# Layer 2's first chunks gather raw rows, moments are taken block by block, table blocks leave the filling, and idle TensorE multiplies for nobody

## The chip, the cores and the metric

One core of a Trainium2 chip runs the whole kernel. The core has five engines that work side by side, each through its own instruction queue and in order: PE (TensorE, matrix products and transposes), DVE (VectorE), ACT (ScalarE), POOL (GpSimd) and SP (SyncE, which here issues transfers only). The metric is the time of one execution on the device, in microseconds (us).

## The reference

A graph with N = 6250 nodes of D = 128 features and 106,250 edges (50,000 in both directions and one loop per node), sorted by destination. Two layers of a graph transformer with two heads are applied, with a batch normalisation and a ReLU between them, and the result is added to the input and normalised:

```python
def _transformer_conv(h, edge_attr, src, dst, Wq, bq, Wk, bk, Wv, bv, We, Ws, bs):
    q = (h @ Wq + bq).reshape(n, H, C)
    k = (h @ Wk + bk).reshape(n, H, C)
    v = (h @ Wv + bv).reshape(n, H, C)
    e = (edge_attr @ We).reshape(-1, H, C)
    kj = k[src] + e
    alpha = jnp.einsum('ehc,ehc->eh', q[dst], kj) / jnp.sqrt(jnp.asarray(C, h.dtype))
    ...
    a = ex / den[dst]          # softmax over the edges of one destination
    out = jax.ops.segment_sum((v[src] + e) * a[:, :, None], dst, num_segments=n)
    return out.reshape(n, H * C) + h @ Ws + bs
...
rel_t_enc = jnp.cos(rel_t[:, None] * time_w[None, :] + time_b)
edge_attr = jnp.concatenate([rel_t_enc, msg], axis=-1)
h = _transformer_conv(x, edge_attr, ..., Wq1, ...)
mu = h.mean(axis=0)
var = ((h - mu) ** 2).mean(axis=0)
h = jax.nn.relu((h - mu) / jnp.sqrt(var + 1e-05) * bn_g + bn_b)
return _transformer_conv(h, edge_attr, ..., Wq2, ...)
...
x = _layernorm(x + gnn(x, ...), axis=-1)
```

The mean and the variance of the normalisation run over all nodes, so no value of layer 2 can be formed before the last node of layer 1 is done. What can be done before is anything that works on the raw rows h.

## The kernel before

**Chunks.** The edges are cut into 107 chunks (NC) of 1024 edges, each of eight tiles of 128. A chunk covers a window of 64 destination nodes (NN). The function conv(c, extra) does one layer, c = 0 or 1, as a loop over rounds k from -4 to 109. It is a pipeline written out by hand: the program order is the order on every engine. In round k:

- fetch(k+4): SP loads the chunk's edge attributes into the buffer ff (L720) and its part of the table into ftab (L731); in layer 2 also the stored time code, the turned edge features and the residual rows (L734 to L738). DVE fills some columns of ff (L723 in layer 2, L726 to L729 in layer 1).
- gather(k+4): POOL issues eight indirect transfers (L743), each of which fetches the source rows of 128 edges: in layer 1 from xv_d (the input with its time), in layer 2 from h_d (layer 1's rows after normalisation and ReLU).
- score(k), L809/L810: PE multiplies the table by the turned features; lowest(k), L815/L817: DVE takes a bound; weigh(k), L822: ACT's exponential, once in a round.
- turn_weights(k-1), L832/L833, and gather_sums(k-1), L839: the weights are turned (PE, then ACT) and multiply the gathered rows; the sums are in fpa, a single bank.
- divide(k-2), L844 to L847; finish_turn(k-2), L853 to L856; finish(k-2): two products (L863/L864), in layer 1 a DVE addition (L869) and a transfer of the 64 columns into hT, the layer's result, which lies in SBUF with the features on partitions; in layer 2 L887 to L891 and the output.
- turn_in(k+1), L792/L793 and for layer 1 L799: PE transposes the gathered rows, ACT copies them.
- in layer 1, encode and sine form the time code of a chunk two or three rounds ahead (L760 to L768 on DVE, a sine on ACT), place copies it into ff (L779).
- pull(extra, 1): one step of side work.

Buffers of a chunk (ff and ftab) are there six times, so the gathers of a layer's first six chunks can run one after the other, and the seventh waits until the first chunk's sums (L839) have read their buffer. This stretch, rounds -4 to -1, is called the filling here.

**Side work.** A table holds, for a block of 512 nodes, what score needs of the destinations: tables() makes five products of 128x512 (L627), whose results ACT (L631 twice, L629) and DVE (L633 twice) write into fo, and one transfer writes fo, 1.5 MB, to tab_d (L637). There are 13 blocks. In layer 1 block 0 is made before the loop and blocks 1 to 12 are steps of rest(), five to a block, with small loads (load_others) after block 2 and the folded weights of layer 2 (matrices) behind the last. Six steps are pulled in round -4 and one in each round after. In layer 2 a block has the table and the residual (h @ Ws + bs, added to the input, L1030 to L1032, written to res_d).

**Between the layers** (L975 to L1046): POOL clears hT's tail; the sum over the nodes, half on DVE, half on ACT (L983); the squares on ACT (L988); scale and shift; then for each block ReLU with scale and shift on ACT (L1003), four transposes on PE (L1006), a copy on DVE (L1008, four buffers fhr) and a transfer into h_d. Then the tables and residuals of blocks 0 and 1 with one PSUM bank, then conv(1), whose first gathers wait for h_d.

## Time and profile before

| | us |
|---|---|
| median of 9 runs | 2882.65 |
| lowest and highest of them | 2842.16, 2895.57 |
| the profiled execution | 2869.65 |
| its span in the profile | 2867.5 |
| mean granted clock of PE in it | 0.941 of full |
| first and last exponential (L822) of layer 1 | 120.3, 1464.4 |
| last transfer into hT landed | 1477.6 |
| first gather of layer 2 | 1508.1 |
| first and last exponential of layer 2 | 1582.9, 2844.7 |

Times are counted from the start of the span. A group line of the page gives line, engine, operation, output <- input, the count, then busy time, mean ns of one, and the idle time of the engine just before such instructions with what ended most of it. A matmul on PE has a record for its product and one (PEld) for the loading of its weights. An indirect transfer is counted on POOL for the time in which POOL writes its descriptors. The clock row (PEclk) shows in 40 slices which share of its full clock PE was granted.

### The profile page before, as it was taken

How to read it: one execution, taken by the hardware profiler on the slowest of the kernel's cores; microseconds unless marked ns; L12 is line 12 of the kernel's file. 1: busy time of each engine (PE TensorE's matmuls, PEld its weight loads, DVE VectorE, ACT ScalarE, POOL GpSimd, SP SyncE). 2: the span in 40 equal slices, each digit the busy share in tenths (PEclk: the TensorE clock that was granted, in tenths of full speed). 3: DMA queues.
4: the chain of work that ended last, by engine and by line, in shares of the span. 5: the costliest groups of instructions: out<-in, count | busy, mean ns of one | idle time of the engine just before them, and what ended most of it. 6: DMA issues, size and time to landing. Idle time of an engine off the chain costs nothing.

```text
span 2867.5 us, 39250 instructions
## 1 busy us (share of the span) xinstructions
PE 2387.0 (83%) x11637; PEld 1761.5 (61%) x11637; DVE 1242.9 (43%) x3735; ACT 1236.2 (43%) x1950; POOL 1636.9 (57%) x1733
## 2 busy tenths in 40 slices
PE   5588898888888888888864989889988888888887
PEld 3366666666666666666651656666666666666665
DVE  3455566555556565655531333333333222232223
ACT  2355665544454444544451334333333333333334
POOL 4355565555556566666606466666666666666661
PEclk7799999999999999999985999999999999999998
DMA  6345555554455455455424555565555454544451
GB/s 196 116 116 146 139 153 149 138 145 139 138 161 143 128 135 134 133 133 134 134 79 133 167 149 160 151 167 150 157 155 151 132 130 129 137 133 133 128 134 48
DMA packets 428354, 396.58 MB, mean 138 GB/s; under 512 B 282064, under 2 KB 371940, under 8 KB 424804
## 3 DMA queue, kind: packets, MB, share of 16 engines
q1 hardware_dynamic: 354406, 238.66, 30.2%
q0 software_dynamic: 55168, 114.12, 16.2%
q10 hardware_dynamic: 18558, 41.20, 4.0%
q8 instruction: 95, 1.56, 0.2%
q14 instruction: 127, 1.04, 0.1%
HBM read 279.72 MB, written 110.59 MB: 136 GB/s over the span
## 4 chain that ended last, share of the span: by engine, by line
PE 33%; issue 6%; another core or an unknown queue 4%; DVE 3%; POOL 2%; DMA 1%; ACT 1%; SPq 0%; DVEq 0%; ACTq 0%; POOLq 0%
PE fpa L839 11%; PE fps L809 5%; PE fps L810 5%; PE fppt L832 3%; PE fpx L792 3%; POOL ff L743 2%; PE fpg L627 1%; PE fpo L875 1%; PE fpo L853 1%; PE fpo L876 1%; DMA ff<-h_d,fsrcs 1%; DVE fa L847 1%; PE fpo L854 0%; DVE flow L815 0%
## 5 line engine op out<-in xcount | busy, mean ns | idle before, releaser
L743 POOL DMA_INDIRECT ff<-xv_d,fsrcs x856 | 821.6, 960 | 596.4 <-issue 224.3
L743 POOL DMA_INDIRECT ff<-h_d,fsrcs x856 | 810.2, 946 | 521.6 <-issue 252.2
L839 PE MATMUL fpa<-ff,fpt 128*128 128x225 f32 x3424 | 709.6, 360 | 0.2
L839 PEld LDWEIGHTS fpa<-ff,fpt 128*128 128x128 f32 x3424 | 641.8, 193 | 13.5 <-issue 0.9
L809 PE MATMUL fps<-fft,ftab 128*128 128x512 f32 x856 | 463.2, 620 | 90.0 <-ACT fs L822 45.3
L793 ACT COPY fft<-fpx 128x512 f32<-128x512 f32 x428 | 250.1, 584 | 527.3 <-PE fpx L792 191.5
L832 PEld LDWEIGHTS fppt<-fident,fs 128*128 128x128 f32 x1712 | 204.5, 141 | 200.2 <-issue 195.1
L832 PE MATMUL fppt<-fident,fs 128*128 128x128 f32 x1712 | 251.3, 276 | 83.0 <-issue 81.0
L833 ACT COPY fpt<-fppt 128x512 f32<-128x512 f32 x428 | 227.1, 581 | 129.0 <-PE fppt L832 55.8
L792 PE MATMUL fpx<-fident,ff 128*128 128x128 f32 x1712 | 261.6, 290 | 14.9 <-DVE fbits L726 13.5
L822 ACT ACTIVATE fs<-fps,fm 128x1024 f32<-128x1024 f32 x214 | 238.7, 1115 | 68.5 <-issue 29.8
L815 DVE TENSOR_REDUCE flow<-fps 128x1 f32<-128x1024 f32 x214 | 260.0, 1215 | 13.3 <-PE fps L810 13.3
L891 ACT ACTIVATE fsq<-fy 64x128 f32<-64x128 f32 x107 | 33.1, 310 | 505.2 <-DVE fy L889 310.4
L887 DVE SCALAR_TENSOR_TENSOR fres<-fpo,fr 64x128 f32<-64x128 f32 x107 | 30.2, 282 | 506.5 <-PE fppt L832 196.2
L809 PEld LDWEIGHTS fps<-fft,ftab 128*128 128x128 f32 x856 | 170.8, 228 | 127.8 <-issue 67.1
L810 PE MATMUL fps<-fxT,ftab 112*128 112x512 f32 x428 | 228.9, 613 | 6.2 <-issue 5.4
L792 PEld LDWEIGHTS fpx<-fident,ff 128*128 128x128 f32 x1712 | 216.9, 151 | 20.1 <-DVE fbits L726 15.1
L810 PE MATMUL fps<-fet,ftab 112*128 112x512 f32 x428 | 222.8, 601 | 0.3 <-issue 0.3
L799 ACT COPY fet<-fpe 112x512 f32<-112x512 f32 x214 | 126.5, 591 | 223.4 <-PE fppt L832 80.4
L856 DVE COPY fat<-fpo 128x256 f32<-128x256 f32 x214 | 90.9, 425 | 254.6 <-PE fpo L854 107.8
L853 PEld LDWEIGHTS fpo<-fident,fa 128*128 128x128 f32 x214 | 30.8, 144 | 269.3 <-issue 155.1
L853 PE MATMUL fpo<-fident,fa 128*128 128x128 f32 x214 | 65.6, 307 | 139.2 <-DVE fa L847 92.6
(198 smaller groups left out, 2549.8 us busy)
## 6 DMA issues: line engine op xcount, KB each, us to landing
ff<-in_edge_attr SPq DMA_DIRECT2D x214, 256.0 KB
et_d<-fet SPq DMA_DIRECT2D x107, 448.0 KB
fxT<-et_d SPq DMA_DIRECT2D x107, 448.0 KB
ftab<-tab_d SPq DMA_DIRECT2D x107, 192.0 KB
tab_d<-fo ACTq DMA_DIRECT2D x13, 1536.0 KB
ff<-xv_d,fsrcs POOLq DMA_INDIRECT x856
enc_d<-fzs SPq DMA_DIRECT2D x107, 128.0 KB
ff<-h_d,fsrcs POOLq DMA_INDIRECT x856
```

Of the source, the lines that this page charges most:

```text
L743: nc.gpsimd.indirect_dma_start(out=f[:, t, (1 if c else 0):1 + D], out_offset=None, in_=h_d if c else pl.xv_d, in_offset=bass.IndirectOffs ...
L792: nc.tensor.transpose(px[:, t * P:(t + 1) * P], s.f[:, u * 4 + t, 1:1 + D], ident)
L793: nc.scalar.copy(s.ft[:, u * GE:(u + 1) * GE], px)
L799: nc.scalar.copy(s.et[:, u * GE:(u + 1) * GE], pe[:EC])
L809: nc.tensor.matmul(s.ps[:, w], s.tab[:, :, 0], s.ft[:, w], start=True, stop=False)
L810: nc.tensor.matmul(s.ps[:, w], s.tab[:EC, :, 1], s.et[:, w], start=False, stop=True)
L815: nc.vector.tensor_reduce(low, s.ps, AX.X, OP.min)
L822: nc.scalar.activation(s.s, s.ps, AF.Exp, bias=s.bias, scale=-1.0)
L832: nc.tensor.transpose(pp[:, t * P:(t + 1) * P], s.s[:, at:at + P], ident)
L833: nc.scalar.copy(s.pt[:, u * GE:(u + 1) * GE], pp)
L839: nc.tensor.matmul(s.pa, s.pt[:, t * P:(t + 1) * P], s.f[:, t, 1:1 + D + EW], start=t == 0, stop=t == T - 1)
L853: nc.tensor.transpose(s.po[:, 0], s.a[:, :D], ident)
```

## The change

**Raw rows.** While layer 1 still runs, the finished columns of hT are turned into rows and written to h_d before any normalisation (pass_rows: four transposes, a DVE copy, one transfer per block; a block is passed when no later chunk can write to it, by the test on at_round: blocks 0 to 9 in rounds 84 to 92, block 10 in round 100, blocks 11 and 12 in rounds 108 and 109). The chunks 0, 1 and 2 of layer 2 (RAW = 3) gather these raw rows. For them turn_in applies the ReLU with scale and shift in ACT's copy out of PSUM, and normalise(k) does the same to the rows in ff with three DVE operations over 128x1024, by a tile (spread) that holds scale and shift along the free axis, made with two products. All other chunks gather from a second buffer, hn_d, which first_blocks writes: the ReLU of blocks 1 to 12, then for all 13 blocks transposes, copy and transfer. It stands in layer 2's round -4, behind fetch(0) and gather(0).

**Moments.** In pass_rows DVE takes bn_stats of the block; bn_aggr joins the 13 results, in place of the two passes over hT.

**Tables.** No step is pulled before round 0. From there one in a round, two in rounds 0 to 3 and from 81 on. Each block has two steps more that hold nothing or one of the small loads; the rows follow as further steps. fo and fzs have one buffer instead of two. In layer 2 only block 0 is made ahead of the loop, with three banks; the blocks 1 to 12, each with two empty steps, are steps of the rounds.

**Products that nobody reads.** keep_busy(n) issues n products of 128x225 on PE: 8 near the start of the plan (the index work before the layers), 12 behind the first table, 24 in round -1 of either layer ahead of turn_in(0), and 24 each in rounds 108 and 109 of layer 1. Those of round 108 stand ahead of finish(106), the layer's last chunk.

The memset of hT's tail moves to the start. The diff, cut:

```diff
 def tables(nc, pl, c, fT, b0, work, bank):
-    o = work.tile([P, GE, H, 3 - c], F32, name="fo", tag="fo")
+    o = work.tile([P, GE, H, 3 - c], F32, name="fo", tag="fo", bufs=1)
     for i, (a, b) in enumerate(pl.mats[c]):
...
     h_d = dram.tile([N, D], F32, name="h_d")
+    hn_d = dram.tile([N, D], F32, name="hn_d")
+    at_round = [0]
+    stats = const.tile([P, -(-N // GE), 6], F32, name="fstats")
     res_d = dram.tile([NP, D], F32, name="res_d")
     enc_d = dram.tile([NC, P, T * TD], F32, name="enc_d")
...
     SINGLE = 24
-    def conv(c, extra):
+    RAW = 3
+    def conv(c, extra, first_blocks=None):
         cs = ExitStack()
...
                 nc.gpsimd.indirect_dma_start(
-                    out=f[:, t, (1 if c else 0):1 + D], out_offset=None, in_=h_d if c else pl.xv_d,
+                    out=f[:, t, (1 if c else 0):1 + D], out_offset=None, in_=(h_d if k < RAW else hn_d) if c else pl.xv_d,
                     in_offset=bass.IndirectOffsetOnAxis(ap=pl.srcs[:, t, k:k + 1], axis=0))
         shape = [P, T, TD]
...
             args.clear()
-            z = work.tile([P, 2, T, TD], F32, name="fzs")
+            z = work.tile([P, 2, T, TD], F32, name="fzs", bufs=1)
             nc.scalar.activation(z[:, :len(of)], arg[:, :len(of)], AF.Sin, bias=qpi)
             turned.extend((k, z[:, i]) for i, k in enumerate(of))
...
                 nc.tensor.transpose(px[:, t * P:(t + 1) * P], s.f[:, u * 4 + t, 1:1 + D], ident)
-            nc.scalar.copy(s.ft[:, u * GE:(u + 1) * GE], px)
+            if c and k < RAW:
+                nc.scalar.activation(s.ft[:, u * GE:(u + 1) * GE], px, AF.Relu, bias=pl.shift, scale=pl.scale)
+            else:
+                nc.scalar.copy(s.ft[:, u * GE:(u + 1) * GE], px)
             if c:
...
             nc.vector.tensor_scalar(s.a, s.pa, inv, None, op0=OP.mult)
+        def normalise(k):
+            rows = ch[k].f[:, :, 1:1 + D]
+            for i, op in enumerate((OP.mult, OP.add)):
+                nc.vector.tensor_tensor(rows, rows, pl.spread[:, None, i].to_broadcast([P, T, D]), op)
+            nc.vector.tensor_scalar(rows, rows, 0.0, None, op0=OP.max)
         def finish_turn(k):
             s = ch[k]
...
             if j > NC - 3:
                 nc.sync.dma_start(tail_d[bass.ds(at - base, NN), :], o)
+        def keep_busy(n):
+            idle = p_a.tile([P, D + EW], F32, name="fpa")
+            for _ in range(n):
+                nc.tensor.matmul(idle, ident, pl.even, start=True, stop=True)
         def pull(gen, n):
...
                     gather(k + AHEAD)
-                if k == -AHEAD and c == 0:
-                    pull(extra, 6)
+                if k == -AHEAD and c:
+                    first_blocks()
                 if on(k):
...
                     lowest(k)
+                if k == -1 or c == 0 and k > NC:
+                    keep_busy(24)
                 if on(k + 1):
...
                             sine()
-                pull(extra, 1)
+                if k >= 0:
+                    at_round[0] = k
+                    pull(extra, 2 if k < 4 or k > 80 else 1)
                 if len(args) == 3 or args and k == NC - 4:
...
                 if c and on(k):
+                    if k < RAW:
+                        normalise(k)
                     nc.vector.tensor_copy(ch[k].f[:, :, 1 + D:1 + D + TD], ch[k].z)
...
                     gather_sums(k - 1)
+            at_round[0] = 2 * NC
             for _ in extra:
...
             turn_features(nc, pl, mp, N)
+        def pass_rows(b0):
+            r0 = b0 * GE
+            n = min(GE, N - r0)
+            rows = turned_rows(b0)
+            nc.vector.bn_stats(stats[:, b0], hT[:, r0:r0 + n])
+            yield
+            put_rows(h_d, b0, rows)
+            yield
+        def turned_rows(b0):
+            r0 = b0 * GE
+            n = -(-min(GE, N - r0) // P)
+            pt = pl.bank().rearrange("p (b d) -> p b d", d=P)
+            for i in range(n):
+                nc.tensor.transpose(pt[:, i], hT[:, r0 + i * P:r0 + (i + 1) * P], ident)
+            rows = pw.tile([P, GE // P, P], F32, name="fhr")
+            nc.vector.tensor_copy(rows[:, :n], pt[:, :n])
+            return rows
+        def put_rows(to, b0, rows):
+            r0 = b0 * GE
+            n = min(GE, N - r0)
+            full = n // P
+            if full:
+                nc.sync.dma_start(to[r0:r0 + full * P, :].rearrange("(b p) d -> p b d", p=P), rows[:, :full])
+            if n > full * P:
+                nc.sync.dma_start(to[r0 + full * P:N, :], rows[:n - full * P, full])
         def rest():
+            others = load_others(nc, pl, const, conv2, bn_g, bn_b)
             for b0 in range(1, NT):
                 yield from tables(nc, pl, 0, xT[:, b0 * GE:(b0 + 1) * GE], b0, pw, lambda: pl.bank())
-                if b0 == 2:
-                    yield from load_others(nc, pl, const, conv2, bn_g, bn_b)
+                for _ in range(2):
+                    next(others, None)
+                    yield
             yield from matrices(nc, pl, 1, const, lambda: pl.bank()[:, :P])
+            for b0 in range(-(-N // GE)):
+                while at_round[0] < 3 + max(k for k in range(NC) if first(k)[0] < (b0 + 1) * GE):
+                    yield
+                yield from pass_rows(b0)
         conv(0, rest())
-    nc.gpsimd.memset(hT[:, N:], 0.0)
-    with tc.tile_pool(name="fbn1", bufs=1) as one, tc.tile_pool(name="fbnw", bufs=2) as pw:
-        neg = one.tile([P, 2], F32, name="fmu")
-        half = N // 2
-        scr = pl.xT
-        nc.vector.tensor_reduce(neg[:, 0:1], hT[:, :half], AX.X, OP.add)
-        nc.scalar.activation(scr[:, half:N], hT[:, half:N], AF.Copy, accum_out=neg[:, 1:])
-        mu = one.tile([P, 1], F32, name="fmu1")
-        nc.vector.tensor_add(mu, neg[:, 0:1], neg[:, 1:])
-        nc.vector.tensor_scalar(mu, mu, -1.0 / N, None, op0=OP.mult)
-        var = one.tile([P, 1], F32, name="fbvar")
-        nc.scalar.activation(scr[:, :N], hT[:, :N], AF.Square, bias=mu, accum_out=var)
-        nc.vector.tensor_scalar(var, var, 1.0 / N, EPS, op0=OP.mult, op1=OP.add)
-        nc.scalar.activation(var, var, AF.Sqrt)
-        scale = one.tile([P, 1], F32, name="fscale")
-        nc.vector.reciprocal(scale, var)
+        moments = const.tile([P, 2], F32, name="fmom")
+        nc.vector.bn_aggr(moments, stats)
+        std = const.tile([P, 1], F32, name="fstd")
+        nc.vector.tensor_scalar(std, moments[:, 1:], EPS, None, op0=OP.add)
+        nc.scalar.activation(std, std, AF.Sqrt)
+        scale = pl.scale = const.tile([P, 1], F32, name="fscale")
+        nc.vector.reciprocal(scale, std)
         nc.vector.tensor_mul(scale, scale, pl.bng)
-        shift = one.tile([P, 1], F32, name="fshift")
-        nc.vector.tensor_mul(shift, scale, mu)
-        nc.vector.tensor_add(shift, shift, pl.bnb)
-        NB = -(-N // P)
-        with tc.tile_pool(name="fbnh", bufs=4) as hp, \
-                tc.tile_pool(name="fbnp", bufs=2, space=bass.MemoryType.PSUM) as pps:
-            for b0 in range(0, NB, 4):
-                n = min(4, NB - b0)
-                cs_ = slice(b0 * P, b0 * P + GE)
-                nc.scalar.activation(hT[:, cs_], hT[:, cs_], AF.Relu, bias=shift, scale=scale)
-                pt = pps.tile([P, 4, P], F32, name="fpt")
-                for i in range(n):
-                    nc.tensor.transpose(pt[:, i], hT[:, (b0 + i) * P:(b0 + i + 1) * P], ident)
-                hr = hp.tile([P, 4, P], F32, name="fhr")
-                nc.vector.tensor_copy(hr[:, :n], pt[:, :n])
-                full = min(n, (N - b0 * P) // P)
-                if full:
-                    nc.sync.dma_start(h_d[b0 * P:(b0 + full) * P, :].rearrange("(b p) d -> p b d", p=P), hr[:, :full])
-                if full < n:
-                    left = N - (b0 + full) * P
-                    nc.sync.dma_start(h_d[(b0 + full) * P:N, :], hr[:left, full])
+        shift = pl.shift = const.tile([P, 1], F32, name="fshift")
+        nc.vector.tensor_mul(shift, scale, moments[:, 0:1])
+        nc.vector.tensor_sub(shift, pl.bnb, shift)
         def residual(b0):
...
             next(res, None)
             yield
-        with tc.tile_pool(name="fpp2", bufs=1, space=bass.MemoryType.PSUM) as pp:
+        def relu(b0):
+            r = slice(b0 * GE, (b0 + 1) * GE)
+            nc.scalar.activation(hT[:, r], hT[:, r], AF.Relu, bias=shift, scale=scale)
+        def first_blocks():
+            for b0 in range(1, NT):
+                relu(b0)
+            for b0 in range(-(-N // GE)):
+                put_rows(hn_d, b0, turned_rows(b0))
+        with tc.tile_pool(name="fpp2", bufs=3, space=bass.MemoryType.PSUM) as pp, tc.manual_schedule():
             pl.bank = lambda: pp.tile([P, GE], F32, name="fpg")
-            for b0 in range(2):
-                for _ in block(b0):
-                    pass
+            relu(0)
+            for _ in block(0):
+                pass
+            diag = const.tile([P, 2, P], F32, name="fdiag")
+            spread = pl.spread = const.tile([P, 2, P], F32, name="fspread")
+            pb = pp.tile([P, 2, P], F32, name="fpb", bufs=1)
+            for i, col in enumerate((scale, shift)):
+                nc.vector.tensor_scalar(diag[:, i], ident, col, None, op0=OP.mult)
+                nc.tensor.matmul(pb[:, i], pl.ones, diag[:, i], start=True, stop=True)
+            nc.vector.tensor_copy(spread, pb)
         def rest():
-            for b0 in range(2, NT):
+            for b0 in range(1, NT):
                 yield from block(b0)
-        conv(1, rest())
+                yield
+                yield
+        conv(1, rest(), first_blocks)
     nc.sync.dma_start(out[N - NN:N, :], tail_d[NN:2 * NN, :])
...
         got.hT = keep.tile([P, NP], F32, name="fhT")
+        nc.gpsimd.memset(got.hT[:, N:], 0.0)
         got.rest = keep.tile([P, 1 + D], F32, name="fxrest")
         got.raw, got.web, got.ws, got.mats = {}, {}, {}, ([], [])
...
         nc.vector.tensor_scalar(nxt, jpp[:, :NC], 1.0, None, op0=OP.is_equal)
-        ones = pl.tile([P, P], F32, name="pones")
-        nc.vector.memset(ones, 1.0)
+        even = got.even = keep.tile([P, D + EW], F32, name="pones")
+        nc.vector.memset(even, 1.0)
+        ones = got.ones = even[:, :P]
         ends = pl.tile([1, 2, NC + 1], F32, name="ends")
...
         got.lanes = lane_i
+        def keep_busy(n):
+            idle = pp.tile([P, D + EW], F32, name="one", tag="one", bufs=1)
+            for _ in range(n):
+                nc.tensor.matmul(idle, even[:, :P], even, start=True, stop=True)
+        keep_busy(8)
         winf = pl.tile([R, P], F32, name="winf")
...
             pass
+        keep_busy(12)
         columns(flats[0], srcs)
...
```

## The prediction, made before the changed kernel had run

> **What bounds the kernel now.** I read the page first: the busy shares, the chain that ended last, the costliest groups; then the exponentials of a few stretches, which give the time of a round; then two rounds on POOL; then the table of windows around the two places where the rounds stop.
>
> ```profile
> PE 2387.0 (83%) x11637; PEld 1761.5 (61%) x11637; DVE 1242.9 (43%) x3735; ACT 1236.2 (43%) x1950; POOL 1636.9 (57%) x1733
> ...
> PEclk7799999999999999999985999999999999999998
> ...
> L743 POOL DMA_INDIRECT ff<-xv_d,fsrcs x856 | 821.6, 960 | 596.4 <-issue 224.3
> L743 POOL DMA_INDIRECT ff<-h_d,fsrcs x856 | 810.2, 946 | 521.6 <-issue 252.2
> ```
>
> PE is busy 83% of the span, but POOL's gathers come at a fixed step: 0.95 us and 0.30 us of issue, so eight of a chunk take 10 us. The two dips in the clock row are the filling of layer 1 and the change of layers. The exponential L822 runs once a round; here it is in rounds with tables in them, in late rounds of layer 1 without, and in layer 2:
>
> ```profile
> L822 ACT ACTIVATE fs<-fps,fm x26: 1114/1116/1132, 407.9 to 746.6; 128x1024 f32<-128x1024 f32 x26
> ...
> L822 ACT ACTIVATE fs<-fps,fm x47: 1114/1114/1122, 899.0 to 1454.6; 128x1024 f32<-128x1024 f32 x47
> ...
> L822 ACT ACTIVATE fs<-fps,fm x17: 1114/1114/1120, 2205.0 to 2397.1; 128x1024 f32<-128x1024 f32 x17
> ```
>
> (746.6 − 407.9)/25 = 13.55 us a round with tables, (1454.6 − 899.0)/46 = 12.08 without, 192.1/16 = 12.01 in layer 2. POOL's timeline of layer 2 shows what the 12 are: a burst of eight, then 2.4 us for a buffer that PE must release.
>
> ```profile
> 2001.81 0.95 POOL L743 DMA_INDIRECT ff<-h_d,fsrcs  x1 [0.31 <-issue]
> 2005.13 0.95 POOL L743 DMA_INDIRECT ff<-h_d,fsrcs  x1 [2.37 <-PE fppt L832]
> ```
>
> So within a round only what lengthens that last 2 us counts, and what starts the rounds earlier counts fully. The windows (span, then busy time of PE, PEld, DVE, ACT, POOL, granted clock, DMA share, GB/s):
>
> ```profile
> 1478.00:1490.00 12.00, 0.02 (x1) 0.02 (x1) 1.11 (x7) 10.62 (x8) 0.12 (x1) 0.50 0.00 0
> 1490.00:1506.00 16.00, 10.68 (x51) 6.71 (x51) 8.46 (x13) 9.56 (x13) 0.00 (x0) 0.82 0.68 200
> 1506.00:1530.00 24.00, 15.81 (x22) 5.27 (x22) 4.85 (x8) 3.47 (x3) 16.69 (x18) 0.50 0.58 165
> 1530.00:1570.00 40.00, 13.04 (x28) 6.06 (x28) 3.63 (x5) 2.90 (x3) 28.71 (x31) 0.59 0.45 129
> ```
>
> The statistics are 12 us of ACT alone; then the rows; then 48 gathers without a pause (1508.1 to 1567.9) while PE works at half clock. The last hT write lands at 1477.6, the first sums of layer 2 (L839) are done at 1590.3, and the seventh chunk's gathers wait for exactly that. In the filling of layer 1 the same: 48 gathers from 38.4 to 98.2, then POOL waits until 131.3 for the first sums (127.8).
>
> **The change, part by part**, against the profiled execution: 2869.65 us (span 2867.5). The median of the runs shown is 2882.65, 13 more; the sum is carried over to it.
>
> *Filling of layer 1.* Ten pulls of tables go. They kept DVE in one wait:
>
> ```profile
> 102.51 1.12 DVE L633 SCALAR_TENSOR_TENSOR fo<-fpg,fb,fcode 128x512 f32<-128x512 f32 x1 [20.90 <-remote]
> ```
>
> Behind it stood encode(0) (104.1 to 107.5), its sine, placing and transposes; first exponential 120.3. Freed, encode(0) runs when its rows land, near 50. What is late next is the hand-over from PE to ACT and DVE: under the gathers such waits end late, in the change of layers by 3.7, 3.7, 11, 16 and 22 us, so I let the copies of chunk 0 (L793) end near 100 instead of 112.7, and the sums 14 us earlier: **−14**. Bounds: 0, if it all clears only when another buffer moves, and −30, if POOL's whole pause of 33 us goes but for one chain. The 24 products before it (22 behind the features' products) take 9.65 us at full clock, by eight of 128x225 in 3.21 us (L839), 19 at half clock, inside the same wait: 0.
>
> *Rounds of layer 1.* The ten pulls reappear in rounds, at 13.55 − 12.08 = 1.47 each: **+15**; 0 if the blank pulls and the early double ones absorb them. The passing of raw rows comes in ten rounds (84 to 92, and 100) that now run at 12.08: four transposes 0.60 on PE, a copy 0.69 on DVE and bn_stats (not in the trace; between a 128x512 add, 0.69, and the 128x1024 reduction, 1.22), ahead of L869 on DVE, thus ahead of a hT write. At most the price of a pull each, +15, at least 0; I take half, **+7**. SP gets a write more of 0.7 us in each: it has 4 rounds of slack. One table buffer (fo, fzs) instead of two: the blank pulls cover the 4 us of a table's write; 0, bounds 0 to +5.
>
> *Eight and twelve products at the start.* 3.2 and 4.8 us on a PE that idles most of 0 to 40; the twelve stand ahead of nothing but products whose inputs come later: 0, bounds −2 to +5.
>
> *Change of layers*, as one line of times. The 24 products of round 108 stand before L863/L864 of the last chunk (1474.5): +9.65, the last hT write lands at 1487.3 and not 1477.6. The 24 of round 109 run on to 1493.4; the last transposes 0.6, copy 0.7, write 2.5 to 4 (h_d writes took 2.4 to 4.2): raw rows complete at 1498. Beside them bn_stats, bn_aggr, the square root with its table (1.48) and five small DVE steps of 0.16 put the shift at 1498 too, after 1489.0 now: the removed L983 (2.81) and L988 (5.50) pay less than the products cost. But POOL starts at 1498 instead of 1508.1: 24 raw gathers, to 1528. Block 0's table, with three banks and a waking clock (a pair of products 1.05, not 2.07), is written at 1507 and there at 1511 (1520.0 now). Then 13 blocks of transposes, copies and hn_d writes with two buffers: 0.9 us a block now with four; with two, each pair waits for a landing, some 1.9 a block, 25 us in all, from 1508, and three to land: 1536. Under the raw gathers DVE's waits on PE grow, by the rows 3.7 a block at the least bad: 13 × 3.7 = 48, 1560 with the landing. I take 1540, nearer the first since the gathers stop at 1528. Fetches of chunks 1 to 5 stand behind the 13 writes on SP; chunks 3 to 5 cannot be gathered before. Behind the transposes PE has 24 products (9.65; 19 at half clock), from 1538 to 1548, then chunk 0: transposes 1.2, ACT 0.6, scores 2.5, reduction 1.4, exponential with table 2.4, transposes and copies 2.3, sums 3.2: 13.6, to 1562 clean; 24 in the filling (103.7 to 127.8), to 1572. I take 1566, that is **−24** against 1590.3. Bounds: 1545 (hn_d at the present cadence, no lateness), −45; 1600 (1560, then 19 + 24 less the overlap of two or three), +10. Layer 2's tables of block 1 and later move into rounds that cost 12.0 with and without them; normalise (three DVE operations of about 1.2) has 8 us of free DVE in a round: 0, bounds 0 to +8.
>
> Sum: −14 + 15 + 7 − 24 = −16: 2854 in the profiled execution, **2866** at the median.
>
> The Trainium skill bears on the products (TensorE: Matmul & The Clock Gate, What's actually happening): about 3.4 us of sustained work lifts the clock, an idle window of the same length drops it. The trace's halves agree (0.50 in 1506 to 1530, pairs of 2.07). It speaks against this change: after the filling's and layer 2's products PE waits for ACT and DVE longer than that, so the clock falls before the sums; I estimate from the page that 24 products then take 11.4 us, and the sum stays. On normalise, SBUF — State Buffer (SBUF: two separate sides) has DVE operations with two SBUF inputs shut out GpSimd work that reads SBUF; a gather took 960 ns in layer 1 beside encode's such operations and 946 in layer 2, so the row gives 14 ns.
>
> **Rivals.** *More is won* (0.28): filling −30, the ten pulls and the rows hidden (0), the change of layers −40: −70, 2813. For it: POOL's 33 us pause is visible, and layer 2 hides its tables. Against: layer 1 did not hide them, and 19 us of products stand at its end.
>
> *The start is not earlier* (0.14): the filling clears with the 48 gathers as now (0), pulls +15, rows +7, change −24: −2; or with the filling's −14 and no gain at the change: +8. 2881 to 2891. For it: what ended first in both burst places was the end of the burst.
>
> *Slower* (0.22): the hn_d queue. SP holds chunk 1's fetch, POOL chunk 3's gathers, and PE its 24 products behind 13 two-buffered writes under a burst. It decides from hn_d being complete at about 1560 (1560 + 30 us of gathers is today's 1590). At 1600 for the sums (+10), with +15 and +15 in layer 1 and nothing at the filling: +40, 2923. For it: waits that grew to 22 us there; against: the burst is half as long.
>
> *The forecast* (0.36): 2846 to 2890.
>
> **The numbers.** 1%, 29 us, is what a measurement of this kernel can tell from none (2853.8 to 2911.5 is within). Faster: all of the first rival and a third of the forecast, 0.28 + 0.12 = 0.40. Within: 0.24 of the forecast, 0.12 of the second rival, 0.01 of the third: 0.37. Slower: 0.02 + 0.21 = 0.23. The range leaves 0.1 of the first and 0.1 of the slower rival outside: 2802 to 2922.
>
> **What would show it.** First exponential of layer 1 near 106 (120.3 now); rounds of 12 to 13.5 lasting to round 83; rounds 84 to 92 at 12.7; from the last sums of layer 1 (1472.7) to the last hT write 14.6 us (4.9 now), to the first gather of layer 2 25 (35.4 now), to its first sums 93 (117.6 now); hn_d's last write before POOL's 25th gather. I am wrong if bursts of gathers delay hand-overs otherwise than now, or if rounds can go below 12 us.

## The result

The changed kernel is slower. Its median is 2909.6 us (10 runs, 2896.4 to 2922.9) against 2880.3 us of the kernel before (31 runs); the ratio is 1.0152, with a 95% interval of 1.0120 to 1.0185. The forecast was 2866, a gain of 0.6%. The time lies inside the stated 2802 to 2922, but the sign is wrong.

The profiled execution took 2883.7 us (span 2881.8), less than any other run of this kernel, so its profile holds only 14 us of the loss. A second profile of the same kernel (c1 below) has a span of 2937.3; of this difference of 55.5 us, 45.5 lie in rounds 30 to 80 of layer 1, although the kernel is the same. Single rows are therefore trusted here where they come back in several profiles, and sizes are taken from ratios of medians.

### The profile page after: what moved, and what is told of

Same layout as the page of the kernel before. It is cut to its first block, busy times and chain, and to the rows that moved or that the text cites. A ratio compares the mean times of both kernels' runs of the same rounds, so it can differ in the third digit from the quotient of the medians.

```text
span 2881.8 us, 39871 instructions
## 1 busy us (share of the span) xinstructions
PE 2428.6 (84%) x11922; PEld 1813.0 (63%) x11922; DVE 1259.4 (44%) x3771; ACT 1227.2 (43%) x1946; POOL 1637.0 (57%) x1733
## 4 chain that ended last, share of the span: by engine, by line
PE 33%; another core or an unknown queue 6%; issue 5%; DVE 4%; POOL 1%; DMA 1%; ACT 1%; DVEq 0%; SPq 0%; POOLq 0%; ACTq 0%
PE fpa L847 10%; PE fps L817 5%; PE fps L818 5%; PE fppt L840 4%; PE fpx L797 3%; PE fpg L627 2%; POOL ff L748 1%; PE fpo L889 1%; PE fpa L925 1%; PE fpo L867 1%; DVE flow L823 1%; PE fpo L890 1%; DMA ff<-hn_d,fsrcs 1%; DVE fa L855 1%
## 5 line engine op out<-in xcount | busy, mean ns | idle before, releaser
L748 POOL DMA_INDIRECT ff<-hn_d,fsrcs x832 | 788.5, 948 | 494.7 <-issue 211.2
L817 PE MATMUL fps<-fft,ftab 128*128 128x512 f32 x856 | 466.7, 622 | 67.5 <-issue 33.6
L823 DVE TENSOR_REDUCE flow<-fps 128x1 f32<-128x1024 f32 x214 | 260.0, 1215 | 36.8 <-remote 22.6
L830 ACT ACTIVATE fs<-fps,fm 128x1024 f32<-128x1024 f32 x214 | 238.7, 1116 | 61.0 <-issue 22.2
```

The lines of the kernel that those rows point to most:

```text
L748: nc.gpsimd.indirect_dma_start(out=f[:, t, (1 if c else 0):1 + D], out_offset=None, in_=(h_d if k < RAW else hn_d) if c else pl.xv_d, in_o ...
L817: nc.tensor.matmul(s.ps[:, w], s.tab[:, :, 0], s.ft[:, w], start=True, stop=False)
L823: nc.vector.tensor_reduce(low, s.ps, AX.X, OP.min)
L830: nc.scalar.activation(s.s, s.ps, AF.Exp, bias=s.bias, scale=-1.0)
```

## The profile after

The page of the changed kernel, the lines that answer to those shown of before:

```profile
PE 2428.6 (84%) x11922; PEld 1813.0 (63%) x11922; DVE 1259.4 (44%) x3771; ACT 1227.2 (43%) x1946; POOL 1637.0 (57%) x1733
...
PEclk7799999999999999899997999999999999999999
...
L748 POOL DMA_INDIRECT ff<-xv_d,fsrcs x856 | 820.6, 959 | 607.1 <-PE fpa L847 232.2
L748 POOL DMA_INDIRECT ff<-hn_d,fsrcs x832 | 788.5, 948 | 494.7 <-issue 211.2
```

PE has 42 us more to do and the second dip of the clock is shallower, but POOL's gathers take the same 0.95 us and wait as much as before, in layer 1 now for PE's sums. Where they wait more is read from the exponential, L822 in the kernel before and L830 now. The first 31 rounds of layer 1 in the kernel before, and then in the changed kernel; there also the five exponentials around round 82, and rounds of layer 2:

```profile
L822 ACT ACTIVATE fs<-fps,fm x31: 1114/1114/1128, 120.3 to 516.1; 128x1024 f32<-128x1024 f32 x31
```

```profile
L830 ACT ACTIVATE fs<-fps,fm x31: 1114/1114/1121, 119.4 to 536.8; 128x1024 f32<-128x1024 f32 x31
...
L830 ACT ACTIVATE fs<-fps,fm x5: 1114/1115/1120, 1158.8 to 1220.8; 128x1024 f32<-128x1024 f32 x5
...
L830 ACT ACTIVATE fs<-fps,fm x17: 1114/1115/1120, 2199.5 to 2394.5; 128x1024 f32<-128x1024 f32 x17
```

Three things are in these lines. The first exponential comes at 119.4 where it came at 120.3: the empty filling brought next to nothing. The first 30 rounds take 417.4/30 = 13.9 us where they took 13.2. And around round 82 the four rounds take 62.0/4 = 15.5, where late rounds of layer 1 took 12.1. In layer 2 rounds take 12.2 (12.0 before, 12.1 in both over longer stretches).

What ACT waits for in rounds 10 to 20 (waiting instruction, awaited one, total us, times, longest) is a wait that the kernel before does not have:

```profile
ACT L779 <- DMA enc_d<-fzs: 27.2, 10, 5.4
```

L779 is the sine. It writes fzs, a chunk's time code, and with one buffer it may start only when the time code of the last chunk has been transferred to enc_d. Behind it in ACT's order stand the copies that the next products need.

The filling of layer 1, on the timeline of PE and ACT: the 24 products (L925; a product of this type has two records), then chunk 0's transposes and the first copy of them.

```profile
58.82 6.84 PE L925 MATMUL fpa<-pones,fident 128*128 128x225 f32 x26
...
85.58 0.53 PE L925 MATMUL fpa<-pones,fident 128*128 128x225 f32 x1 [2.28 <-issue]
...
101.66 0.53 PE L925 MATMUL fpa<-pones,fident 128*128 128x225 f32 x1 [2.26 <-issue]
...
108.99 1.06 PE L797 MATMUL fpx<-fident,ff 128*128 128x128 f32 x4
...
110.14 0.59 ACT L801 COPY fft<-fpx 128x512 f32<-128x512 f32 x1 [29.47 <-PE fpx L797]
```

The first 26 records take 6.8 us; from 67 us on, in the midst of POOL's 48 gathers, one record comes every 2 to 3 us, seldom faster or slower, though the profile shows nothing that PE waits for ("issue"). The products that were to fill a wait last until 109 us and are themselves what chunk 0 waits for.

The change of layers, first in the kernel before (the last sums of layer 1, chunk 0's sums in layer 2, the seventh chunk's first gather), then in the changed kernel (timeline of PE, POOL and DVE):

```profile
1469.34 3.21 PE L839 MATMUL fpa<-ff,fpt 128*128 128x225 f32 x16
...
1590.27 3.20 PE L839 MATMUL fpa<-ff,fpt 128*128 128x225 f32 x16
...
1593.74 0.94 POOL L743 DMA_INDIRECT ff<-h_d,fsrcs  x1 [25.88 <-PE fpa L839]
```

```profile
1482.23 3.21 PE L847 MATMUL fpa<-ff,fpt 128*128 128x225 f32 x16
...
1486.71 9.29 PE L925 MATMUL fpa<-pones,fident 128*128 128x225 f32 x48
...
1496.72 9.29 PE L925 MATMUL fpa<-pones,fident 128*128 128x225 f32 x48
...
1509.72 0.94 POOL L748 DMA_INDIRECT ff<-h_d,fsrcs  x1 [68.11 <-ACT fhT L1082]
...
1560.32 0.95 POOL L748 DMA_INDIRECT ff<-hn_d,fsrcs  x1 [20.68 <-DMA hn_d<-fhr]
...
1594.59 1.23 DVE L823 TENSOR_REDUCE flow<-fps 128x1 f32<-128x1024 f32 x1 [22.62 <-remote]
...
1598.49 3.21 PE L847 MATMUL fpa<-ff,fpt 128*128 128x225 f32 x16
...
1601.97 1.03 POOL L748 DMA_INDIRECT ff<-hn_d,fsrcs  x1 [11.36 <-PE fpa L847]
```

The last sums of layer 1 end at 1485.4. Then twice 24 products, 9.29 us each, on the path; the 24 raw gathers begin at 1509.7; POOL stands from 1539.6 to 1560.3 for hn_d; the next 24 gathers run to 1590.6, and DVE, idle since 1572, begins on chunk 1's scores at 1594.6, though PE's last product for them ends at 1576.7 ("remote" in a row: the profile has no record of what ended the wait). The sums of chunk 0 end at 1601.7 and release the seventh chunk at 1602.0, 116.5 us after the last sums of layer 1. In the kernel before the same way took 121.2 us (1472.55 to 1593.74). In the second pair of profiles the order is turned: 118.4 in c1 and 116.9 in c2.

## The experiments

Eighteen runs followed the first. The sessions they were made in are of two kinds, called A and B here. In A the kernel before takes 2790 to 2880 us and rounds of layer 2 take 12 us, as in the profiles above; in B it takes 2332 to 2336 us and these rounds take 10.1, POOL's bare step of eight times 1.25. The chip number on record does not sort them: 13 stands for e1 to e4, which are B, and for the runs d and g, which are A. So whether the chip or something else of the session makes the kind is not shown. All ratios are to the kernel before in the same session. Between two sessions of kind A the ratio of one and the same kernel differed by 0.9% (c3 and g2), so differences within a session weigh more.

| run | kernel | kind | ratio (95%) |
|---|---|---|---|
| first | changed | A | 1.0152 (1.0120 to 1.0185) |
| c1 | changed | A | 1.0174 (1.0132 to 1.0217) |
| f1 | changed | B | 1.0309 (1.0292 to 1.0327) |
| e1 | two fzs buffers | B | 1.0044 (1.0027 to 1.0061) |
| f2 | the same | B | 1.0036 (1.0021 to 1.0050) |
| g1 | the same | A | 0.9935 (0.9891 to 0.9980) |
| e2 | without the 48 products at the end | B | 1.0239 (1.0222 to 1.0256) |
| e3 | without the 24 of round -1 | B | 1.0310 (1.0293 to 1.0327) |
| e4 | double pulls from round 88 | B | 1.0273 (1.0256 to 1.0290) |
| f3 | the same | B | 1.0275 (1.0258 to 1.0292) |
| f4 | two fzs buffers, double pulls from 88 | B | 1.0001 (0.9992 to 1.0011) |
| c4 | before, one fzs buffer | A | 1.0053 (1.0001 to 1.0104) |
| d1 | without any products | A | 1.0073 (1.0038 to 1.0108) |
| c3 | f4 and without any products | A | 0.9858 (0.9820 to 0.9895) |
| g2 | the same | A | 0.9773 (0.9704 to 0.9841) |
| d2 | c3, hn_d written by ACT's queue | A | 0.9869 (0.9816 to 0.9922) |
| d3 | c3, tables in the filling | A | 0.9860 (0.9806 to 0.9914) |
| d4 | d2, six chunks raw | A | 0.9917 (0.9885 to 0.9950) |

c2 is a look at the kernel before (2864.3 us). Its first exponential is at 118.1, its rounds 30 to 40 take 12.1 us and 50 to 60 14.0, where the first profile has 13.7 and 12.6: the same rounds move by more than a microsecond from one execution to the next.

> The changed kernel itself once more, as the measure for the other runs. On the chip of the last four runs the kernel before took 2331.7 us and rounds of layer 2 took 10.14 us, POOL's bare step of eight times 1.25, where the first profiles had 12. Theory A (the parts add up): about 2400 us on such a chip, 1.03 of before; on one like the first, 1.015. Theory B (the parts overlap): what e1 to e4 saved comes out at less than the sum of their differences.

> The changed kernel as the measure of f2 to f4: 1.015 to 1.02 of before on a chip with rounds of 12 us in layer 2, about 1.03 on one with 10.

> The kernel before, for a profile on the chip of these runs. On a chip like that of the last four runs: rounds of 10.1 to 10.5 us throughout, waits of DVE and ACT on PE under a burst of gathers below 1 us, first exponential of layer 1 near 75, and some 85 to 100 us from the last exponential of layer 1 to the first of layer 2. On a chip like the first: the rows of the first profile.

### Two buffers for the time code (e1, f2, g1), and one in the kernel before (c4)

```diff
-            z = work.tile([P, 2, T, TD], F32, name="fzs", bufs=1)
+            z = work.tile([P, 2, T, TD], F32, name="fzs")
```

> The changed kernel with two buffers for fzs again, nothing else. Theory A (the single buffer costs layer 1's first 24 rounds: ACT's sine waits for the transfer of the last time code, 27.2 us in ten waits in rounds 10 to 20 of the changed kernel): those rounds come back from 15.1 to about 13.0 us, the whole is 20 to 27 us shorter than the changed kernel. Theory B (the rounds are paced by the gathers and the tables, the wait only replaces another one): within 8 us of the changed kernel.

> The changed kernel with two fzs buffers. Theory A (the wait of ACT on the transfer of the last time code is the larger loss, on any chip): 1.2 to 1.8% below f1 where rounds take 12 us, 2.5% where they take 10; rounds 0 to 30 of layer 1 about 12 (or 10.5) us. Theory B (under slow hand-overs the wait hides behind others, as in c4): 0.3 to 0.8% below f1.

> The changed kernel with two fzs buffers. Where rounds take 12 us: theory A (the wait is a loss on any chip) 1.000 to 1.006 of before, after 1.015 and 1.017 with one buffer; theory B (it hides there) 1.009 to 1.014. Where they take 10: 1.004 as in e1 and f2.

> The kernel before with one buffer for fzs, nothing else. Theory A (the single buffer is a cost of its own): the first 24 rounds of layer 1 get 2 to 2.7 us longer each, the whole 50 to 65 us on a chip with rounds of 10 us, 20 to 27 on one like the first. Theory B (it costs only beside the new order of the tables): below 10 us.

In B, f1 against f2 in one session is 2407.6 − 2344.5 = 63 us, 2.6%, and e1's 1.0044 agrees; e1's own theories had expected less (20 to 27 us, or under 8). In A the ratio goes from 1.0152 and 1.0174 to 0.9935, by 2.2 to 2.4% or 63 to 69 us, but these are three sessions. Within one session there are d1, with one buffer, at 2810.2 us, and d2 and d3, with two buffers and single pulls up to round 87, at 2754.2 and 2751.3 (each has one more change, told below): 56 to 59 us less, of which the pulls account for some 10 (rounds 80 to 90 take 130.0 us in d1, 119.9 and 119.4 in d2 and d3). That leaves 46 to 49 us for the buffer, 1.7%: the upper end of what theory A expected in A. The waits of the sine in f1 over the first 26 rounds (what its engine sat idle for; total us, times), and then the first 31 exponentials of g1:

```profile
  DMA enc_d<-fzs: 102.6, 23
```

```profile
L830 ACT ACTIVATE fs<-fps,fm x31: 1113/1114/1120, 118.7 to 478.6; 128x1024 f32<-128x1024 f32 x31
```

g1's first 30 rounds take 359.9/30 = 12.0 us, the changed kernel's 13.9 (14.0 in c1). With two buffers neither f2's nor g1's sine has such a wait. The same rounds within one session, in d1 (one buffer) and d3 (two), and then in c3 (two):

```profile
L830 ACT ACTIVATE fs<-fps,fm x31: 1114/1114/1125, 108.3 to 503.9; 128x1024 f32<-128x1024 f32 x31
```

```profile
L830 ACT ACTIVATE fs<-fps,fm x31: 1114/1114/1117, 115.1 to 474.8; 128x1024 f32<-128x1024 f32 x31
```

```profile
L830 ACT ACTIVATE fs<-fps,fm x31: 1113/1114/1129, 111.9 to 529.2; 128x1024 f32<-128x1024 f32 x31
```

13.2 us a round against 12.0, and c3 does not fit: two buffers, no wait of the sine for a transfer, and still 13.9. Its profiled execution, 2856.4 us, is the longest of its runs (median 2829.5); what lengthened these rounds there is not known. So the sign and the wait are shown, in B with the size, while the size in A, 46 to 69 us, rests on medians. It is enough to turn a gain (0.65% in g1) into the loss of 1.5 to 1.7%.

In the kernel before one buffer costs 0.5% (c4, interval 0.0 to 1.0), some 15 us, which lies between its two theories. The first 30 rounds of the kernel before take 13.2 us with two buffers where g1's take 12.0, 36 us less in all. What makes these rounds of the kernel before long, and hides most of the wait there, the runs do not separate; d3 below excludes the tables of the filling. The other tile that was cut to one buffer, fo, kept it in every run of the changed kernel, so its price was not measured.

### Products (e2, e3, d1)

```diff
-                if k == -1 or c == 0 and k > NC:
+                if k == -1:
                     keep_busy(24)
```

This is e2; e3 has `if c == 0 and k > NC:` in its place, and d1 leaves out all of these and the 8 and 12 at the start.

> The changed kernel without the 48 products of rounds 108 and 109. Theory A (they stand on the path at their full length, 9.3 us twice): the last transfer into hT and the first gather of layer 2 come 9 and 19 us earlier against the last sums of layer 1, and the whole is 15 to 20 us shorter. Theory B (they keep PE's clock up and so shorten block 0's table and the transposes): products of the table at half clock, pairs of 2.07 instead of 1.35 us, and the whole 0 to 10 us shorter.

> The changed kernel without the 24 products of round -1 of both layers. Theory A (under the burst of gathers PE issues the later ones at 2.3 to 2.8 us each, so in layer 1 they hold turn_in(0) from 64 to 109 us): first exponential of layer 1 between 85 and 110 us instead of 119.4, and in layer 2 the first scores 10 us earlier; the whole is 15 to 35 us shorter. Theory B (all hand-overs clear only when the burst has ended at 101.5, whatever PE has done before): first exponential at 108 to 119, the whole 0 to 12 us shorter.

> The changed kernel without any of the products that nobody reads; one fzs buffer and the double pulls stay. Theory A (products lie on the path: 18.6 us at the end of layer 1, and in the filling they hold turn_in(0) until the burst has ended): 20 to 35 us shorter than the changed kernel, so between 0.995 and 1.01 of before. Theory B (they buy clock): no shorter than 10 us.

e2 saves 0.7% beside f1, some 16 us, theory A's lower end (both are B, in two sessions): the time from the last exponential of layer 1 to the seventh of layer 2 goes from 138.4 us (f1) to 124.4. e3 saves nothing in B (1.0310 and 1.0309): its first exponential comes at 69.1 instead of 74.4 and the seventh of layer 2 3.1 us earlier after layer 1, but from the first to the last exponential of layer 1 it takes 1180.3 us instead of 1173.1 (the first ten rounds 13.1 us each instead of 12.7). In B the 24 products of the filling run through, as f1's PE timeline shows, 22 of them without a break:

```profile
56.12 10.16 PE L925 MATMUL fpa<-pones,fident 128*128 128x225 f32 x44
```

They cost more in A: without any products the first exponential comes at 108.3 (d1; 111.9 and 112.0 in c3 and g2) and not at 119.4 and 120.0, and the same stretch between the layers is 151.7 us, not 177 and 179. Most of the delay against B's 69 to 75 us for the first exponential stays without them. The ratio 1.0073 is 0.8 to 1.0% below the changed kernel's in other sessions. Within one session g1 and g2, which differ in the products and the double pulls, are 46.5 us apart (2857.3 and 2810.8), 14 of which lie in rounds 80 to 90 (134.0 and 120.2 us). No run gave a gain for the products.

### Double pulls (e4, f3, f4)

```diff
-                    pull(extra, 2 if k < 4 or k > 80 else 1)
+                    pull(extra, 2 if k < 4 or k > 87 else 1)
```

> The changed kernel with double pulls from round 88 and not from 81, so that the seven steps of the folded weights come one to a round. Theory A (two of these steps in a round make a chain PE, DVE, PE twice in it, 19.2 us a round in rounds 82 and 83): rounds 80 to 90 go from 13.45 to 12.1 to 12.5, the whole is 8 to 14 us shorter. Theory B (it is the raw rows that these rounds carry): the time moves to the rounds after 88 and the whole is within 5 us.

> The changed kernel with double pulls from round 88 on. Theory A: rounds 80 to 90 at 12.0 instead of 13.0 to 13.5, 0.3 to 0.5% below f1. Theory B (double pulls matter more than two rounds show): 0.8% or more.

> Both undone, the products stay. Theory A (they lie in different rounds and add up): the sum of f2's and f3's differences within 0.4%; against c3, which is this without the products, 0.7 to 1.2% longer, so 0.992 to 0.998 of before. Theory B: less than the larger of the two differences plus a third of the other.

From round 81 the steps pulled are not yet the raw rows but the folded weights of layer 2, each a chain from PE to DVE and back; two in one round made rounds 82 and 83 of the changed kernel 19 us long in A (23 and 16 in c1). f3 is 0.34% (9 us) below f1, and rounds 80 to 90 go from 11.0 to 10.3 us. f4 is 71 us below f1, f2 and f3 alone 63 and 9: the two add up, theory A; but the ratio of 0.992 to 0.998 that was expected with it was not reached (1.0001). The raw rows, which now fall into rounds 88 and later, leave hardly a trace: rounds 88 to 100 take 10.16 us, 10.06 in f1.

### What is left of the change (c3, g2), and its parts (d2, d3, d4)

c3 and g2 are the changed kernel with two fzs buffers, double pulls from round 88 and no products.

> The changed kernel with two buffers for fzs, double pulls from round 88 on, and none of the products that nobody reads (8, 12, 24, 24, 48); raw rows, moments by block and the empty filling stay. Theory A (these three were the losses): 85 to 95 us shorter than the changed kernel on a chip like that of the last four runs, thus 15 to 25 us faster than before. Theory B (the raw rows with the writes to hn_d cost as much as they bring): within 10 us of before.

> The version with the three parts undone (c3). Where rounds take 10 us: 18.6 us of products at the end of layer 1 and up to 10 in the fillings less than f4, so 0.988 to 0.993 of before under theory A (raw rows, moments and filling gain on any chip); 0.996 to 1.000 under theory B (they gain only where hand-overs are slow). Where rounds take 12: 0.986 as in c3.

It beats both kernels: the kernel before by 1.4% and 2.3% in two sessions, and the changed one by 92 us in one session (2921.7 in c1, 2829.5 in c3). So these three parts together were the loss. Between the layers g2 takes 156.2 us from the last exponential to the seventh of layer 2, where the kernel before took 182.9 and 178.8; the first exponential is 6 to 8 us earlier. The first of these is what raw rows, moments by block, one table block ahead of the loop, three banks and the place of the hn_d writes bring together; they were not separated. The largest part lies elsewhere: from the first to the last exponential of layer 1 g2 takes 1293.5 us, the kernel before 1344.1 and 1340.3, with 35 us of it in the first 30 rounds. c3's longer execution does not show this (1356.7), and what makes these rounds shorter was not separated either.

d2 takes c3 and lets ACT issue the writes to hn_d:

```diff
-                put_rows(hn_d, b0, turned_rows(b0))
+                put_rows(hn_d, b0, turned_rows(b0), nc.scalar)
```

> The version with the three parts undone (c3), with its 13 hn_d writes issued by ACT and not by SP, so that the fetches of chunks 1 to 5 stand behind no copy. Theory A (the queue of SP makes chunk 1 late): the first two rounds of layer 2, 19.9 and 19.2 us in c3, become 8 to 12, and the whole is 8 to 18 us shorter than c3. Theory B (the second burst of 24 gathers makes the hand-overs late, whenever the fetches come): the same within 5 us.

The same as c3 in the ratio, theory B. The first two rounds of layer 2 take 7.2 and 34.3 us (19.9 and 19.2 in c3), and the stretch between the layers is longer, 165.9 us. POOL's 25th gather, which waits for hn_d, begins 67.5 us after the last sums of layer 1; in c3, g2 and d3, which write from SP's queue, it is 60.0 to 61.7. SP's loads of edge attributes for chunks 0 to 4 in d2, on the timeline:

```profile
1391.02 0.41 SPq L725 DMA_DIRECT2D ff<-in_edge_attr  x1
...
1416.30 0.70 SPq L725 DMA_DIRECT2D ff<-in_edge_attr  x1
...
1430.47 0.40 SPq L725 DMA_DIRECT2D ff<-in_edge_attr  x1
1438.69 0.41 SPq L725 DMA_DIRECT2D ff<-in_edge_attr  x1
1447.82 0.40 SPq L725 DMA_DIRECT2D ff<-in_edge_attr  x1
```

From chunk 1 on a fetch of five loads takes 8 to 14 us; in the changed kernel, where SP begins them with the second burst, the first takes 4.1 (1559.04 to 1563.15) and the third 12.2 (1570.95 to 1583.10). Of d2's fetches chunk 1's lies in a burst (gathers from 1396.0 to 1425.6), and its steps take 0.7 us each. Those of chunks 2 and 3 lie in POOL's pause after it; there SP waits for transfers into hn_d, up to 4.1 us at a time. So the fetches are slow for more than one reason, and freeing SP's queue did not help.

d3 takes c3 and pulls ten steps in the filling:

```diff
+                if k < 0 and c == 0:
+                    pull(extra, 7 if k == -AHEAD else 1)
```

> The version c3 with ten pulls of tables in the filling again (seven in round -4, one in each of rounds -3 to -1). Theory A (pulls in rounds cost 1.2 to 1.5 us each, in the filling they lie under the gathers but hold DVE): first exponential 8 us later, 120 instead of 112, rounds 10 to 15 us shorter in sum: within 10 us of c3. Theory B (the empty filling is a gain of its own): 10 to 20 us longer than c3.

The same as c3 and d2 within the intervals, theory A's outcome: the first exponential comes at 115.1, which is 3 us later than in c3 and g2 and 7 later than in d2 (108.3), and layer 1 from first to last exponential takes 1273.2 us, d2's 1269.9. But its reason fails: rounds that no longer carry ten pulls are not 10 to 15 us shorter. Ten table pulls cost about nothing in the rounds. That they are free in the filling is not shown: d3 is as fast as d2 only because d2's stretch between the layers is 10 us longer (165.9 and 155.6).

d4 takes d2 and lets all six chunks of the filling be raw:

```diff
-    RAW = 3
+    RAW = 6
```

> d2 with RAW = 6: all six chunks of layer 2's filling gather raw rows, so POOL waits for hn_d only before the seventh; DVE normalises three chunks more. Theory A (POOL's stop for hn_d, 15 to 20 us, is on the path): layer 2's seventh chunk starts 10 to 20 us earlier against the last sums of layer 1. Theory B (a longer burst makes the copies and hand-overs later by as much): within 5 us of d2.

0.9917, not below d2 (0.9869, the intervals overlap): theory B rather than theory A. The stretch between the layers grows from 165.9 to 170.8 us although POOL gathers 48 times without a stop: the first exponential of layer 2 comes 107.3 us after the last of layer 1 (81.3 in d2). That the longer burst holds the hand-overs longer fits this; it was not tested apart.

## Why the prediction was wrong, step by step

- **"One table buffer (fo, fzs) instead of two … 0, bounds 0 to +5"**: this is the step that failed. I named the cover for fo, the blank pulls, and let it stand for fzs too, which they do not cover. fzs is written every round until round 23 and read by a transfer. It cost 63 us in B and 46 to 69 us in A. The question of the buffer's reader, and of what stands behind the writer on ACT, was not asked. With this term at its measured size the sum has the right sign.
- **Filling, −14**: measured −1 at the first exponential and +1 at the end of chunk 0's sums (132.0 against 131.0). The 24 products were costed at "19 at half clock, inside the same wait: 0". In the burst nearly all of them took from 58.8 to 109.2 us, and became the wait. Without products the first exponential was 7 to 12 us earlier, near the size forecast. Where nothing delayed them 24 took 9.29 us (end of layer 1) and 10.65 (round -1 of layer 2), less than the estimate of 11.4.
- **Ten pulls in rounds, +15**: about 0 (d3 against d2). The 1.47 us were the difference of two stretches of one execution; single stretches differ that much between executions of one kernel (c2). With two buffers the first 30 rounds even took 36 us less than in the kernel before (g1), which no term foresaw.
- **Raw rows in rounds, +7**: about 1; rounds 85 to 92, which carry most of them, take 12.2 in the changed kernel (97.3 us for eight) and 12.0 before. What does cost there was not in the sum: the folded weights two to a round, +15 us in rounds 80 to 90 of both profiles of the changed kernel (13.4 a round against 12.0), 9 us in B.
- **Change of layers, −24**: −5 in the first pair of profiles and +1 in the second at the end of chunk 0's sums, 0 to −6 at the seventh exponential. The recorded 1590.3 and 127.8, called the time when sums are done, are where they start: before, chunk 0's sums of layer 2 run from 1590.27 to 1593.5. The clean 1562 behind the forecast counts the 3.2 us of these sums in, so like for like up to 3 us more were promised. The products at the end cost what was forecast (9.29 twice), and the first gather came 24.3 us after the last sums (25 forecast). hn_d was complete 75 us after them, not 67; the sums ended at 116, not 93, since I charged a hand-over (a result of one engine reaching the next) under the second burst with no more than in the filling, while DVE sat idle for 22.6 us in it and ACT for 14.4.
- **The slower rival** had named the right place at the change of layers: its 1560 for hn_d is 87 us after the last sums of layer 1, and the measured 75 lie between it and the forecast's 67. Its price of +10 was too high, and its total, 2923, comes near the measured 2909.6 by luck: the time code's buffer is not in it.
- **normalise, 0**: nothing here speaks against it. Single gathers beside its DVE operations took up to 1.50 us in the changed kernel and 1.56 in f1 instead of 0.95, one to a chunk.
- The 2854 of the sum is 0.994 of the kernel before, and g1's ratio is 0.9935. They agree by luck. The gains counted on at the filling and the change of layers hardly came in g1 (its first exponential is at 118.7, and 180.2 us pass between the layers), and layer 1's rounds, which were to cost 22 us more, took 17 less from first to last exponential (1326.9 against 1344.1).

## What to carry to other kernels

A pool cut from two buffers to one is not priced by its writer alone: list who reads the tile last, with transfers among the readers, and which queue the writer then blocks. Work put into a wait must be cheap under the conditions of that wait; here the place that looked idle was the one where issuing was slowest. A step that costs something per round should be read from several executions before it is put into a sum, and two kernels should be compared in one session.

## What was not expected

In sessions of kind A the issue of PE and SP is slow and signals come late while POOL sends gathers without a pause. PE gets a record every 2 to 3 us where the same products take 10.2 us for 44 records in B. The starts of these records in the filling (67.36, 68.76, 71.56, 73.66, 76.46 and on) lie apart by multiples of 0.70 us, and 0.70 us is also what SP's steps take late in the second burst (1586 to 1590 in the changed kernel). Chunk 1's scores reach DVE 17.9 us after PE's last product for them (1576.7 and 1594.6), and all clears some 4 us after the last gather (1590.6, 1594.6). Late signals are not confined to these places. In every profile of kind A the engines wait 370 to 690 us in all, 120 to 190 times and all through the execution, until something that the profile finds no record for; the rows call it "remote". In the eight profiles of kind B there is not one such wait, the products of the filling run through, rounds of layer 2 fall from 12.1 to 10.1 us, and the kernel before takes 2332 us instead of 2880, while POOL's step between gathers is 1.25 us in both. What makes the kinds differ, and what resource the gathers take, is open; nothing here was run to tell it. The single fzs buffer costs in both: 63 us in B, 46 to 69 in A.
